# Two-layer GNN kernel: the first half of Wk read in its own rows and transposed by TensorE, and the start's ScalarE and VectorE work in another order

## The chip, the cores and the metric

One core of a Trainium2 chip (trn2). The metric is the time of one execution on the device in microseconds; a kernel's time is the median of its runs. Engines are named as in the profile: PE is TensorE, PEld its weight loads, DVE VectorE, ACT ScalarE, POOL GpSimd, SP SyncE. A `q` behind an engine's name (SPq, ACTq, POOLq) is its sequencer, which issues DMAs, among other things.

## The reference

```python
# x (32, 512, 512), adj (32, 512, 512), nodemask (32, 512) of ones; W0 (512, 1024), Wqk (512, 1024), Wv (512, 512)
# layer 0
h = relu(layernorm(x))
agg = einsum('bij,bjf->bif', adj, h) / max(sum(adj, -1), 1e-6)
x = x + relu(concat([h, agg], 2) @ W0.T)
# layer 1
h = relu(layernorm(x))
q, k = split(h @ Wqk, 2, axis=-1)
v = h @ Wv
a = einsum('bij,bjd->bid', adj, k * mask[:, :, None])
w = mask * einsum('bid,bid->bi', q, a) / sqrt(512)
x = x + softmax(w, axis=1)[:, :, None] * v
```

Everything is float32. q . (adj k) needs Wq and Wk only as M = Wq Wk^T (512 x 512), which the kernel computes once at its start.

## The kernel before

Each of the 32 samples is 512 x 512. Products of 512 x 512 by 512 x 512 are done with seven block products of 256 x 256 instead of eight (`left_sums`, `right_sums` and `product` build the sums before and after). The program is one long list in an order written by hand (a manual schedule): each engine carries out its instructions in the order in which the Python code emits them, and the `Plan` objects place side work between the block products of a phase.

`start()` is the opening, for sample 0 and the weights; the main loop over samples 1 to 31 follows. In `start()`:

- `make_identity` on GpSimd (a memset and an affine select) writes the 128 x 128 identity that TensorE's transposes multiply by. `still` is a zeroed tile for the spare matmuls, five of 128 x 512, which give TensorE work while the weights are on their way.
- DMAs are issued from SP and, where `two_queues` is given, in turn from SP and ACT. `exchange` reads a matrix in pieces of 32 rows, four DMAs (one for each 32 partitions), so that VectorE's 32 x 32 block transposes (`turn_natural`, `turn_ordered`, `turn_right`) make the full transpose of it. Order of issue: Wk's first half (`swk_0`), the four quarters of Wq (`swq_0` to `swq_3`), Wk's second half (`swk_1`), x of sample 0 in two halves, the right half of W0 (`sw2_0`, `sw2_1`), all from both queues; then adj of sample 0 (`fa.load`) and the left half of W0 (`sw1`) from SP alone.
- VectorE, in this order: turn of Wk's first half into `wkT`, of the four quarters of Wq into `wqT`, of Wk's second half; statistics of x's four row chunks (`statistics`, `variance` with its power on GpSimd, `shift`), two chunks and their variance at a time; four turns of W0's right half into `w2R`.
- TensorE: the spare matmuls; M as `multiply(d, h)`, d the row block of 128 and h the half of the columns: (0,0), (1,0), (2,0), (3,0), (0,1), (1,1), (2,1); the transposes of the first two chunks of h = relu(layernorm(x)) (`turn_chunk`); (3,1); then layer 0's first product, `layer0_y(0)`, whose tile is `pp_y`.
- ScalarE: its DMA issues; then `place_m(0)`, `normal(0)`, `normal(1)`, `place_m(1)`, copies of the transposed chunks (`keep_chunk`), and so on. `normal(c)` is relu(x * rstd + nmr), the layernorm of one chunk. Its activation table is loaded ahead of its first activation, `place_m(0)`.

A float32 matmul is carried out as two instructions ("halves"), so a `multiply` is four matmuls and eight halves; a float32 transpose is one instruction. The contraction index of M may be in any order, so long as `wqT` and `wkT` have the same.

Of the kernel before, what the change touches and what calls it, by code (L numbers as in the profile page):

```python
# [16 lines left out]
P = 128  # L17
# [5 lines left out]
def kernel(  # L23
# [11 lines left out]
    nc = tc.nc  # L35
    B, N, F = x.shape
    C = N // P
    H = F // 2
    Q = 4
    R = 32  # L40
# [26 lines left out]
    def mm_tile(name):  # L67
        return ps_m.tile([P, 2, H], F32, tag="m", name=name)
# [10 lines left out]
    def copy(o, i):  # L79
        nc.scalar.activation(o, i, AF.Copy)  # L80
# [107 lines left out]
    def by_rows(src):  # L188

        t = src.rearrange("(q c r) f -> q r c f", q=Q, c=C)  # L190
        return [t[q] for q in range(Q)]
# [8 lines left out]
    one_queue, two_queues = (nc.sync, nc.sync), (nc.sync, nc.scalar)  # L200

    def half_rows(t, src, h, queues=one_queue):
        for q, rows in enumerate(by_rows(src)):
            queues[q % 2].dma_start(out=t[q * R:(q + 1) * R, :, :], in_=rows[:, 2 * h:2 * h + 2, :])

    def exchange(src, name, t=None, queues=one_queue):


        if t is None:
            t = big.tile([P, 8, P], F32, tag="s", bufs=2, name=name)  # L210
        for q in range(Q):
            queues[q % 2].dma_start(
                out=t[q * R:(q + 1) * R, :, :], in_=src[:, :, ts(q, P)].rearrange("k r j -> r k j")
            )
        return t


    mhalf = const.tile([P, C], F32, name="mhalf")
    nc.vector.memset(mhalf, -0.5)

    X, AT_, DEG, W, Y, H1M, H1T, U, TV, HT = ({} for _ in range(10))
# [4 lines left out]
    def room_x(b):  # L226

        t = xu_tile(f"xu_{b}")
        X[b] = t.rearrange("p (c f) -> p c f", c=C)
        U[b] = t.rearrange("p (k i f) -> p k i f", k=4, i=2)  # L230
# [5 lines left out]
    def norm_tiles(name):  # L236
        k = name[0]
        mv = small.tile([P, C, 2], F32, tag=f"mv{k}", name=f"mv{name}")
        rstd = small.tile([P, C], F32, tag=f"rstd{k}", name=f"rstd{name}")
        nmr = small.tile([P, C], F32, tag=f"nmr{k}", name=f"nmr{name}")  # L240
        return mv, rstd, nmr

    def statistics(src, t, c, name):
        st = small.tile([P, 6], F32, tag="st", bufs=4, name=f"st{name}_{c}")
        nc.vector.bn_stats(st, src)
        nc.vector.bn_aggr(t[0][:, c, :], st)

    def variance(t, a=0, b=C):
        mv, rstd, nmr = t
        nc.vector.tensor_scalar(rstd[:, a:b], mv[:, a:b, 1], LN_EPS, None, op0=ALU.add)  # L250
        nc.gpsimd.tensor_tensor(rstd[:, a:b], rstd[:, a:b], mhalf[:, a:b], op=ALU.pow)  # L251

    def shift(t, a=0, b=C):
        mv, rstd, nmr = t
        nc.vector.scalar_tensor_tensor(
            nmr[:, a:b], mv[:, a:b, 0], -1.0, rstd[:, a:b], op0=ALU.mult, op1=ALU.mult
        )
# [463 lines left out]
    w2R, hT = wide[:, 0:7], wide[:, 7:14]  # L721
    tv = const.tile([P, 2, 2, 14, P], F32, name="tv")

    def weight_source(src):
        return src.rearrange("(k r) j -> k r j", r=R)

    def turn_right(t, h, k, dst):

        nc.vector.transpose(
            dst[:, 2 * k + h, :, :].rearrange("p b (k r) -> p k b r", r=R),  # L730
            t[:, :, ts(k, 2 * R)].rearrange("p k (c r) -> p k c r", r=R),
        )

    def turn_ordered(t, d, dst):

        nc.vector.transpose(
            dst[:, :, ts(d, P)].rearrange("p a (k r) -> p k a r", r=R),
            t.rearrange("p k (a r) -> p k a r", r=R),
        )

    def turn_natural(t, h, dst):

        nc.vector.transpose(
            dst[:, :, ts(h, H)].rearrange("p a (k r) -> p k a r", r=R),
            t.rearrange("p k (a r) -> p k a r", r=R),
        )

    mraw = const.tile([P, C, B], F32, name="mraw")
# [29 lines left out]
    def start():  # L778

        H1T[0] = big.tile([P, 7, 7, P], F32, tag="h1T", bufs=1, name="late")  # L780
        late = H1T[0].rearrange("p s i f -> p (s i f)")
        identity = held["identity"] = late[:, 5120:5248]
        make_identity(nc, identity)
        still = late[:, 5248:5248 + 512]
# [4 lines left out]
        HT[1] = spread[:, 3584:7168].rearrange("p (s b f) -> p s b f", s=7, b=2)  # L789
        w1R = spread[:, 0:3584].rearrange("p (s b f) -> p s b f", s=7, b=2)  # L790

        def rows16(n):
            return room[:, n:n + 2048].rearrange("p (k f) -> p k f", f=P)

        sq, sk, s1 = rows16(0), rows16(2048), rows16(7168)
        wk_rows = weight_source(wqk[:, F:2 * F])
        wq_rows = wqk[:, 0:F].rearrange("(q c r) j -> c q r j", q=Q, c=C)
        exchange(wk_rows[0:8], "swk_0", sk[:, 0:8], two_queues)
        for d in range(C):
            exchange(wq_rows[d], f"swq_{d}", sq[:, 4 * d:4 * d + 4], two_queues)  # L800
        exchange(wk_rows[8:16], "swk_1", sk[:, 8:16], two_queues)
        room_x(0)
        for h in range(2):
            half_rows(X[0][:, 2 * h:2 * h + 2, :], x[0], h, two_queues)
        s2 = []
        for h in range(2):
            s2.append(exchange(weight_source(w0[:, F:2 * F])[8 * h:8 * h + 8], f"sw2_{h}", None, two_queues))
        fa = FA[0] = FrontA(0)
        fa.load(0)
        fa.load(1)  # L810
        exchange(weight_source(w0[:, 0:F]), "sw1", s1)
        fh = FH[1] = FrontH(1)
        wqT = late[:, 0:2048].rearrange("p (c f) -> p c f", c=C)
        wkT = late[:, 2048:4096].rearrange("p (c f) -> p c f", c=C)
        mask_sb, mask_by = late[:B, 4096:4608], late[:B, 4608:5120]

        spare = mm_tile("spare").rearrange("p a f -> p (a f)")
        for n in range(5):
            nc.tensor.matmul(spare, still[:, 0:P], still, start=True, stop=True)

        t = norm_tiles("0_0")
        h0 = hT
# [27 lines left out]
        def place_m(d):  # L850
            place(d, 0, held["m", d].rearrange("p a f -> p (a f)"))

        turn_natural(sk[:, 0:8], 0, wkT)
        for d in range(C):
            turn_ordered(sq[:, 4 * d:4 * d + 4], d, wqT)
        turn_natural(sk[:, 8:16], 1, wkT)
        for h in range(2):
            for c in (2 * h, 2 * h + 1):
                statistics(X[0][:, c, :], t, c, "0_0")
            variance(t, 2 * h, 2 * h + 2)  # L860
            shift(t, 2 * h, 2 * h + 2)
        for h in range(2):
            for k in range(2):
                turn_right(s2[h], h, k, w2R)

        for d in range(C):
            multiply(d, 0)
# [33 lines left out]
        p = Plan()  # L901
# [53 lines left out]
        p = Plan()  # L955
# [52 lines left out]
        f = F1[0] = FrontH1(0)  # L1008
# [9 lines left out]
        p = Plan()  # L1018
# [25 lines left out]
        p = Plan()  # L1044
# [22 lines left out]
    }  # L1067
    with tc.manual_schedule(engines=engines):
        weights, mvR = start()
        post = None  # L1070
        for i in range(1, B):
            more, last = i + 1 < B, i + 1 == B
            f = F1[i] = FrontH1(i)
            p = Plan()
# [40 lines left out]
            if 1 < i and i + 2 < B:  # L1115
                fh = FH[i + 2]
                late = i == 2
# [22 lines left out]
            p = Plan()  # L1140
# [53 lines left out]
            p = Plan()  # L1194
# [40 lines left out]
            if more:  # L1235
                p = Plan()
# [25 lines left out]
        p = Plan()  # L1262
# [11 lines left out]
        p = Plan()  # L1274
# [39 lines left out]
```

## Time and profile before

| | |
|---|---|
| runs | 2264.6, 2262.58, 2265.03 us; median 2264.6 |
| the profiled execution | 2263.74 us; span 2262.0 us, 32862 instructions |
| PE busy | 2253.7 us (100% of the span) |
| PEld busy | 1981.3 us (88%) |
| DVE, ACT, POOL busy | 1913.5 (85%), 1024.9 (45%), 175.6 us (8%) |
| granted TensorE clock | 1.00 |
| DMA | 463.69 MB, mean 205 GB/s |
| first spare matmul | 1.48 us after the span's start |
| first matmul of M (`pm`) | 7.79 us |
| ScalarE's table load | 18.58 us, 1.28 us long |
| first `normal` on ScalarE | 20.37 us |
| first matmul of layer 0's product (`pp_y`) | 24.15 us |

The span runs from the first to the last instruction that the profiler saw. In a view of the timeline each row has the start and the length in us, the engine, the line of the kernel, the operation, its output and input tiles, their shapes and how often it stands there; the bracket at the end is the idle time of the engine before it and what ended that. In a view of waits a row has who waited and for whom: us in total, how many times, the longest. The chain is the work that ended last, followed back from the end: start, us, what.

### The profile page before, as it was taken

The numbers are of one execution on the slowest core, as the hardware profiler recorded it, in microseconds if no ns is written. First come the engines' busy times: TensorE is split into PE (matmuls) and PEld (weight loads), VectorE is DVE, ScalarE is ACT, GpSimd is POOL, SyncE is SP. The second block draws the span as 40 slices with busy tenths as digits, with TensorE's granted clock in tenths as the row PEclk, the third lists the DMA queues.
The fourth block names the chain that finished last, engine by engine and source line by source line (L and its number), as shares of the span: only waits on it lengthen the run. The fifth ranks groups of instructions, "written<-read, shape, count | busy, mean of one in ns | idle before, by whom it ended". The sixth has DMA issues, their size and how long they took to land.

```text
span 2262.0 us, 32862 instructions
## 1 busy us (share of the span) xinstructions
PE 2253.7 (100%) x10526; PEld 1981.3 (88%) x10526; DVE 1913.5 (85%) x3778; ACT 1024.9 (45%) x1895; POOL 175.6 (8%) x261
## 2 busy tenths in 40 slices
PE   9999999999999999999999999999999999999999
PEld 7888888888888888888888888888888888888888
DVE  7988888888888888888888888888888888888776
ACT  4454443445434544434454344543444443445323
POOL 0010000000000000000000000000000000000000
PEclk9999999999999999999999999999999999999999
DMA  9988787888877887877878788888778777887644
GB/s 205 252 233 246 208 208 193 205 222 219 209 200 192 212 227 204 207 198 201 233 207 209 198 199 218 221 205 203 194 211 228 203 208 193 205 231 209 156 120 108
DMA packets 409997, 463.69 MB, mean 205 GB/s; under 512 B 38208, under 2 KB 271680, under 8 KB 405600
## 3 DMA queue, kind: packets, MB, share of 16 engines
q1 hardware_dynamic: 396608, 426.46, 69.3%
q0 software_dynamic: 8928, 32.51, 8.8%
q10 hardware_dynamic: 4288, 2.62, 0.6%
q8 instruction: 83, 1.36, 0.3%
q14 instruction: 90, 0.74, 0.1%
HBM read 293.93 MB, written 167.51 MB: 204 GB/s over the span
## 4 chain that ended last, share of the span: by engine, by line
PE 98%; DMA 1%; SPq 0%; ACT 0%; issue 0%; DVE 0%; DVEq 0%
PE ptv L470 28%; PE pp_o L103 19%; PE pp_y L103 10%; PE pp_u L103 10%; PE pq_o L103 9%; PE pq_y L103 5%; PE pq_u L103 5%; PE pr_o L103 5%; PE pr_y L103 2%; PE pr_u L103 2%; PE pw L521 1%; DMA mv<-in_L_gnn_Wqk_dram 0%; PE pp_v L103 0%; PE pp_t L103 0%; DMA w<-dw 0%; DMA xu<-in_x_dram 0%
## 5 line engine op out<-in xcount | busy, mean ns | idle before, releaser
L470 PE MATMUL ptv<-mv,h1T 128*128 128x256 f32 x2842 | 618.4, 379 | 0.0
L470 PEld LDWEIGHTS ptv<-mv,h1T 128*128 128x128 f32 x2842 | 539.9, 190 | 73.7 <-DVE xu L449 0.4
L74 DVE TENSOR_TENSOR tv<-tv 128x256 f32<-128x256 f32 (+1 forms) x645 | 322.0, 511 | 13.2 <-ACT tv L80 1.5
L80 ACT ACTIVATE tv<-ptv 128x512 f32<-128x512 f32 (+1 forms) x360 | 185.0, 541 | 262.9 <-PE ptv L470 261.9
L103 PE MATMUL pp_u<-h1m,aT 128*128 128x256 f32 x1024 | 241.9, 379 | 0.0
L103 PE MATMUL pp_y<-wide 128*128 128x256 f32 x992 | 234.4, 379 | 0.7 <-ACT y L80 0.7
L103 PE MATMUL pp_o<-y,aT 128*128 128x256 f32 x992 | 234.3, 379 | 0.0
L103 PE MATMUL pp_o<-w,wide 128*128 128x256 f32 x960 | 226.8, 379 | 0.0
L103 PEld LDWEIGHTS pp_u<-h1m,aT 128*128 128x128 f32 x1024 | 194.5, 190 | 26.4
L103 PEld LDWEIGHTS pp_y<-wide 128*128 128x128 f32 x992 | 188.3, 190 | 26.6 <-ACT y L80 1.1
L103 PEld LDWEIGHTS pp_o<-y,aT 128*128 128x128 f32 x992 | 188.4, 190 | 25.6
L103 PEld LDWEIGHTS pp_o<-w,wide 128*128 128x128 f32 x960 | 182.4, 190 | 24.8
L80 ACT ACTIVATE o<-pp_o 128x512 f32<-128x512 f32 x96 | 57.3, 597 | 300.1 <-PE pp_o L103 300.1
L80 ACT ACTIVATE y<-pp_y 128x512 f32<-128x512 f32 x124 | 74.0, 597 | 234.0 <-PE pp_y L103 234.0
L74 DVE TENSOR_TENSOR tv<-ptv,tv 128x512 f32<-128x512 f32 x240 | 139.9, 615 | 43.2 <-PE ptv L470 39.6
L80 ACT ACTIVATE xu<-pp_u 128x512 f32<-128x512 f32 x127 | 75.8, 597 | 193.6 <-PE pp_u L103 193.6
L77 DVE TENSOR_TENSOR h1T<-h1T 128x512 f32<-128x512 f32 (+1 forms) x183 | 158.3, 879 | 1.2
L251 POOL TENSOR_TENSOR rstd<-rstd,mhalf 128x2 f32<-128x2 f32 (+1 forms) x97 | 79.8, 823 | 642.5 <-DVE rstd L250 642.5
L103 PE MATMUL pq_u<-h1m,aT 128*128 128x256 f32 x512 | 121.0, 379 | 0.0
L74 DVE TENSOR_TENSOR tv<-ptv,m_tv 128x512 f32<-128x512 f32 (+1 forms) x120 | 72.1, 623 | 56.6 <-PE ptv L470 55.4
L103 PE MATMUL pq_y<-wide 128*128 128x256 f32 x496 | 117.3, 379 | 0.0
L103 PE MATMUL pq_o<-y,aT 128*128 128x256 f32 x496 | 117.2, 379 | 0.0
(173 smaller groups left out, 3354.7 us busy)
## 6 DMA issues: line engine op xcount, KB each, us to landing
w<-dw SPq DMA_DIRECT2D x217, 256.0 KB, 4.2
a<-in_adj_dram SPq DMA_DIRECT2D x256, 128.0 KB, 3.0
dx<-xu SPq DMA_DIRECT2D x32, 1024.0 KB, 5.0
sh1T<-dh1T SPq DMA_DIRECT2D x256, 128.0 KB, 3.4
shT<-dhT SPq DMA_DIRECT2D x248, 128.0 KB, 6.0
daT<-a SPq DMA_DIRECT2D x124, 256.0 KB, 3.0
xu<-in_x_dram SPq DMA_DIRECT2D x124, 256.0 KB, 5.4
dh1T<-h1m SPq DMA_DIRECT2D x124, 256.0 KB, 3.2
```

The costliest lines, as they stand in the source:

```text
L74: (on or nc.vector).tensor_tensor(o, a, b, op=ALU.add)
L77: (on or nc.vector).tensor_tensor(o, a, b, op=ALU.subtract)
L80: nc.scalar.activation(o, i, AF.Copy)
L103: nc.tensor.matmul(p[:, rc, :], lt[:, LEFT[k], dk, ts(rc, P)], right[:, dk, :], start=first and rc == 0 and dk == 0, stop=True, skip_group ...
L251: nc.gpsimd.tensor_tensor(rstd[:, a:b], rstd[:, a:b], mhalf[:, a:b], op=ALU.pow)
L470: nc.tensor.matmul(banks[n][:, :, ts(i, P)], left[:, LEFT[k], LEFT_IN[j], :], mvR[:, RIGHT[k], RIGHT[j], :, :], start=first and i == 0, st ...
L521: nc.tensor.matmul(banks[n][:, ts(i, P)], left[:, LEFT[k], LEFT_IN[j], :], mvR[:, RIGHT[k], RIGHT[j], which, :], start=first and i == 0, s ...
```

## The change

Wk's first half (256 rows) is read in its own rows, 128 rows to a DMA, one DMA from each queue in place of four. `turn_first_wk` transposes it on TensorE, four transposes of 128 x 128 for each group of 128 rows, each taking every fourth column, and ScalarE copies the two results into `wkT`. It stands in the program behind the issue of Wq's third quarter, and on TensorE ahead of the first `multiply`. Since `wkT` now has every fourth index in a chunk, the turns of Wq and of Wk's second half take the same order ("(r a)" in place of "(a r)"). The spare matmuls are two in place of five. A copy of four numbers on ScalarE, behind the issue of Wq's first quarter, brings the table load there. Wk's second half is turned in two steps. x is read from SP alone, and `sw1` in eight DMAs in place of four. VectorE's statistics are interleaved: the second pair's statistics begin before the first pair's shift, and the second's shift stands behind a turn of W0.

```diff
--- before.py
+++ after.py
@@ -735,14 +735,14 @@
 
         nc.vector.transpose(
             dst[:, :, ts(d, P)].rearrange("p a (k r) -> p k a r", r=R),
-            t.rearrange("p k (a r) -> p k a r", r=R),
+            t.rearrange("p k (r a) -> p k a r", r=R),
         )
 
-    def turn_natural(t, h, dst):
+    def turn_natural(t, h, dst, a, b):
 
         nc.vector.transpose(
-            dst[:, :, ts(h, H)].rearrange("p a (k r) -> p k a r", r=R),
-            t.rearrange("p k (a r) -> p k a r", r=R),
+            dst[:, a:b, ts(h, H)].rearrange("p a (k r) -> p k a r", r=R),
+            t.rearrange("p k (r a) -> p k a r", r=R)[:, :, a:b],
         )
 
     mraw = const.tile([P, C, B], F32, name="mraw")
@@ -789,34 +789,48 @@
         HT[1] = spread[:, 3584:7168].rearrange("p (s b f) -> p s b f", s=7, b=2)
         w1R = spread[:, 0:3584].rearrange("p (s b f) -> p s b f", s=7, b=2)
 
+        wqT = late[:, 0:2048].rearrange("p (c f) -> p c f", c=C)
+        wkT = late[:, 2048:4096].rearrange("p (c f) -> p c f", c=C)
+        spare = mm_tile("spare").rearrange("p a f -> p (a f)")
+        for n in range(2):
+            nc.tensor.matmul(spare, still[:, 0:P], still, start=True, stop=True)
+
+        def turn_first_wk():
+            for n in range(2):
+                p = mm_tile(f"wk_{n}").rearrange("p a f -> p (a f)")
+                for a in range(C):
+                    nc.tensor.transpose(p[:, ts(a, P)], wk_first[:, n, a:512:C], identity)
+                copy(wkT[:, :, ts(n, P)], p.rearrange("p (a i) -> p a i", a=C))
+
         def rows16(n):
             return room[:, n:n + 2048].rearrange("p (k f) -> p k f", f=P)
 
         sq, sk, s1 = rows16(0), rows16(2048), rows16(7168)
         wk_rows = weight_source(wqk[:, F:2 * F])
         wq_rows = wqk[:, 0:F].rearrange("(q c r) j -> c q r j", q=Q, c=C)
-        exchange(wk_rows[0:8], "swk_0", sk[:, 0:8], two_queues)
-        for d in range(C):
+        wk_first = sk[:, 0:8].rearrange("p (n k) f -> p n (k f)", n=2)
+        for n in range(2):
+            two_queues[n].dma_start(out=wk_first[:, n], in_=wqk[ts(n, P), F:2 * F])
+        exchange(wq_rows[0], "swq_0", sq[:, 0:4], two_queues)
+        copy(late[:, 5760:5764], mhalf)
+        for d in range(1, C):
             exchange(wq_rows[d], f"swq_{d}", sq[:, 4 * d:4 * d + 4], two_queues)
+            if d == 2:
+                turn_first_wk()
         exchange(wk_rows[8:16], "swk_1", sk[:, 8:16], two_queues)
         room_x(0)
         for h in range(2):
-            half_rows(X[0][:, 2 * h:2 * h + 2, :], x[0], h, two_queues)
+            half_rows(X[0][:, 2 * h:2 * h + 2, :], x[0], h)
         s2 = []
         for h in range(2):
             s2.append(exchange(weight_source(w0[:, F:2 * F])[8 * h:8 * h + 8], f"sw2_{h}", None, two_queues))
         fa = FA[0] = FrontA(0)
         fa.load(0)
         fa.load(1)
-        exchange(weight_source(w0[:, 0:F]), "sw1", s1)
+        for h in range(2):
+            exchange(weight_source(w0[:, 0:F])[8 * h:8 * h + 8], f"sw1_{h}", s1[:, 8 * h:8 * h + 8])
         fh = FH[1] = FrontH(1)
-        wqT = late[:, 0:2048].rearrange("p (c f) -> p c f", c=C)
-        wkT = late[:, 2048:4096].rearrange("p (c f) -> p c f", c=C)
         mask_sb, mask_by = late[:B, 4096:4608], late[:B, 4608:5120]
-
-        spare = mm_tile("spare").rearrange("p a f -> p (a f)")
-        for n in range(5):
-            nc.tensor.matmul(spare, still[:, 0:P], still, start=True, stop=True)
 
         t = norm_tiles("0_0")
         h0 = hT
@@ -850,18 +864,22 @@
         def place_m(d):
             place(d, 0, held["m", d].rearrange("p a f -> p (a f)"))
 
-        turn_natural(sk[:, 0:8], 0, wkT)
         for d in range(C):
             turn_ordered(sq[:, 4 * d:4 * d + 4], d, wqT)
-        turn_natural(sk[:, 8:16], 1, wkT)
-        for h in range(2):
-            for c in (2 * h, 2 * h + 1):
-                statistics(X[0][:, c, :], t, c, "0_0")
-            variance(t, 2 * h, 2 * h + 2)
-            shift(t, 2 * h, 2 * h + 2)
-        for h in range(2):
-            for k in range(2):
-                turn_right(s2[h], h, k, w2R)
+        for a in range(2):
+            turn_natural(sk[:, 8:16], 1, wkT, 2 * a, 2 * a + 2)
+        statistics(X[0][:, 0, :], t, 0, "0_0")
+        statistics(X[0][:, 1, :], t, 1, "0_0")
+        variance(t, 0, 2)
+        statistics(X[0][:, 2, :], t, 2, "0_0")
+        shift(t, 0, 2)
+        statistics(X[0][:, 3, :], t, 3, "0_0")
+        variance(t, 2, 4)
+        turn_right(s2[0], 0, 0, w2R)
+        shift(t, 2, 4)
+        turn_right(s2[0], 0, 1, w2R)
+        for k in range(2):
+            turn_right(s2[1], 1, k, w2R)
 
         for d in range(C):
             multiply(d, 0)
```

## The prediction

> **What bounds the kernel now.** I read the page's busy times and chain first, then the waits of TensorE, then the timeline of the first 25 us engine by engine, and last the instructions of one GpSimd line.
>
> ```profile
> PE 2253.7 (100%) x10526; PEld 1981.3 (88%) x10526; DVE 1913.5 (85%) x3778; ACT 1024.9 (45%) x1895; POOL 175.6 (8%) x261
> ...
> PE 98%; DMA 1%; SPq 0%; ACT 0%; issue 0%; DVE 0%; DVEq 0%
> ```
>
> TensorE is the chain almost from end to end. Its waits from 24 us to the end:
>
> ```profile
> PE pp_y L103 <- ACT y L80: 0.7, 1, 0.7
> PE pp_o L103 <- DMA w<-dw: 0.3, 1, 0.3
> ```
>
> That is 1.0 us in 2238. So whatever moves the first matmul of layer 0's Y (pp_y, 24.15 us) moves the end by as much, and the change touches only what lies ahead of it. The chain there:
>
> ```profile
> 20.47 1.41 ACT h L831 x2
> 21.88 0.04 issue
> 21.93 0.66 PE h L763 x4
> 22.59 1.73 PE pm L839 x8
> 24.31 1.73 PE pp_y L103 x8
> ```
>
> One product `multiply(d, h)` is 8 matmul halves in 1.73 us (0.216 each). Eight products are 13.8 us; the transposes of two chunks of h are 8 at 0.11, 0.9 us; restarts 0.1. So 14.8 us of work lie between the first pm and pp_y. They took 24.15 - 7.79 = 16.36: 1.6 us were waits, nearly all for `normal` on ScalarE, which issued DMAs until 18.34 and then loaded its table (18.58, 1.28 us).
>
> The weight loads of TensorE's first matmuls show its pace:
>
> ```profile
> 4.20 0.34 PEld L819 LDWEIGHTS spare<-late 128*128 128x128 f32 x1 [0.52 <-issue]
> 5.05 0.31 PEld L819 LDWEIGHTS spare<-late 128*128 128x128 f32 x1 [0.52 <-issue]
> 5.60 0.19 PEld L819 LDWEIGHTS spare<-late 128*128 128x128 f32 x1 [0.24 <-issue]
> 6.03 0.19 PEld L819 LDWEIGHTS spare<-late 128*128 128x128 f32 x1 [0.24 <-issue]
> ```
>
> The halves of the spare matmuls stand 0.85 us apart until 5.05 and 0.43 from 5.60 on: at about 5.3 us, 3.8 after the first (1.48), the pace doubles. (The granted clock reads 1.00 throughout and doesn't show this.)
>
> GpSimd's timeline holds what I take to decide the case:
>
> ```profile
> 0.73 0.20 POOL masks.py:197 MEMSET late<- 128x128 f32 x1 [0.29 <-POOLq L1300]
> 8.97 0.28 POOL masks.py:199 TENSOR_SCALAR_AFFINE_SELECT late<-late 128x128 f32<-128x128 f32 x1 [8.04 <-issue]
> 17.87 0.74 POOL L251 TENSOR_TENSOR rstd<-rstd,mhalf 128x2 f32<-128x2 f32 x1 [8.62 <-DVE rstd L250]
> ```
>
> The identity is complete only at 9.25, though its two instructions are first in the program. Before the change nobody reads it until 21.22. The same pause stands elsewhere; of `Post`'s line 342:
>
> ```profile
> L342 POOLq MODIFY_POOL_CONFIG  x60: 83/83/83, 154.3 to 2168.6; - x60
> ...
>   issue: 144.4, 19
> ```
>
> Behind such a configuration GpSimd sits idle for no visible reason, 144.4 / 19 = 7.6 us each (6.8 to 8.9); the one at the start lies at 1.0 us. I therefore expect the same pause in the changed kernel.
>
> **The change, part by part.** *Wk's first half.* Removed: VectorE's turn of 128x1024 (1.25 us) and two DMAs. Added: 8 transposes on TensorE ahead of the first product, and two copies of 128x512 on ScalarE. `multiply(0, 0)` needs both copies, the copies the transposes, and the transposes the identity. The row of a chunk of h gives 0.11 us for a transpose at full pace, with 0.3 from the last start until its result can be read; at half pace I take 0.22. The copy is 0.60 (ACT L80, 0.597 on the page). The start T0 of the products:
> - identity 9.25, transposes 8 x 0.22 = 1.75 and tail 0.3: 11.3; second copy 0.60: 11.9; wake-ups 0.1: T0 = 12.0.
> - at full pace 8 x 0.11 = 0.9: T0 = 11.15.
> The two DMAs (2 KB rows) and swq_0 land well ahead of 9.25 (the eight transfers first issued had landed by 6.9 us before), so they cost nothing.
>
> *Spare matmuls, 5 to 2.* Four halves of 0.85 end at about 5.0. Then TensorE stands idle for over 4 us. The trace has no such gap, so what the pace is afterwards must be bounded: nothing lost (full pace), or the ramp again. The row's ramp of 3.8 us at half pace costs 1.9; a ramp that has to begin twice over costs 3.8. I take 2.4, above the row, since transposes with waits between them come first. With it pp_y starts at 12.0 + 14.8 + 2.4 = 29.2, that is 5.05 us later than before. Ends for this part: 11.15 + 14.8 = 25.95 (1.8 later) and 30.6 (6.5 later).
>
> [...]
>
> *ScalarE's and SP's queues.* ScalarE issues DMAs in program order with its other work, so behind its two copies stand its issues of swq_3, swk_1 and sw2. At most eight transfers are out at once: the ninth issue, at 4.06, waits for the first to land, and so on down both queues:
>
> ```profile
> SPq L212 <- DMA mv<-in_L_gnn_Wqk_dram: 3.3, 5, 1.5
> ...
> SPq L204 <- DMA mv<-in_L_gnn_Wqk_dram: 2.8, 4, 1.0
> ```
>
> So SP's second transfer of x waits for a piece of swq_3 that ScalarE can issue only at 12.0; it lands some 2.7 us later (median of 64 KB), at 14.7. swk_1 lands at about 16.4, two turns of 0.71 end at 17.9, and `multiply(0, 1)` wants it at 21.4. Seven more transfers of x, 0.9 MB at about 215 GB/s, land at 18 (first half) and 20. Statistics 2 x 0.85, 0.17, GpSimd's 0.74 and the shift give `normal(0)` its operands at 20.5, about when ScalarE's last sw2 issue is through; TensorE wants h at 26.6. Nothing of this reaches the path: the smallest slack is 3.5 us (1.1 at full pace).
>
> *Table load early, statistics in another order.* The load (1.28 us) moves to about 2.2 us beside the first transfers, and VectorE no longer stands 0.86 us twice for GpSimd. Together with the shorter queue they would remove the 1.6 us of waits, and the sum above has them removed already (14.8, not 16.36). If their cover fails, at most these 1.6 us come back.
>
> *Strided reads.* The turns of Wq and the transposes now read every fourth element. No row shows such a read. For VectorE's four turns of 0.71, even double lies beside the wait for the identity, so nothing; for the transposes between nothing and double, 0.9 to 1.75 us; I take nothing, as at half pace there is time to read. *Wk's second half in two turns* (1.42 for 1.25): 0.2 us inside 3.5 of slack. *sw1 in eight issues for four:* about 1.5 us of SP's queue. sw1 was read at 35.25, 3.4 us ahead of its last turn and 4.3 ahead of pp_o (39.5); both now move by about 5 us.
>
> Sum: +5.05 us. The profiled execution took 2263.74 (span 2262.0), 0.86 under the median of 2264.6; so 2268.8 against its own time, 2269.6 against the median.
>
> **Rivals.** *A, the identity is early (not slower).* If GpSimd's pause at the start is a matter of that one execution or of how GpSimd's spans are drawn, transposes start when Wk lands, about 5.2. The copies then follow ScalarE's seventh issue, T0 is about 7.1, (2, 1) ends at 19.3, and h's first chunk comes at 19.75 and the second at 20.4, since ScalarE is still held by sw2's issues until 18.3: pp_y at about 22.7, 1.45 earlier, 2263.1. It decides when the identity is complete before some 7.4 us. Against it: 19 pauses of the same kind in this trace, none under 6.8.
> *B, TensorE keeps full pace* through the gap: T0 11.15, pp_y 25.95, +1.8, 2266.4. For it: the pauses up to 1.25 us before lost nothing. Against: this one is over three times as long, and two spares end before the 5.3 us at which the pace doubled.
> *C, the transfers fall behind as well.* ScalarE's queue stands from about 6.4 to 12, in which some 1 MB less is moved (5 us at 210 GB/s). The stage after is nearly saturated; if adj's halves then come later than TensorE's own delay, ScalarE's sums wait and its copies behind them. Two us more: +7, 2271.6.
>
> **How the numbers follow.** A measurement of this kernel can tell about 0.2% (4.5 us) from no change. Forecast 0.66, of which 0.1 has a loss of pace small enough to stay under 4.5; C 0.05; B 0.17; A 0.10; something faster that I don't see 0.02. Slower: 0.56 + 0.05, about 0.60; same: 0.38; faster: 0.02. The range runs from B with the identity 1 us earlier (2265.4) to the forecast with the longest pause (+0.9) and the longest ramp (+1.4), 2272.0; outside lie A and the unseen.
>
> **What would show it.** Right: the affine select near 9 us and the first transpose of Wk behind it, waiting for GpSimd; the first pm at 11 to 12, its halves 0.43 apart for some us; ScalarE's swq_3 issue at about 12; pp_y near 29. Wrong: transposes before 7 us, or pm halves at 0.216 from the first.

## The result, and the profile after

The changed kernel takes 2268.45 us in the median of 22 runs, the kernel before 2264.2 in 22: 4.25 us more, a ratio of 1.0018 with a 95% interval of 1.0012 to 1.0024. The profiled execution took 2267.56 us, its span 2265.8.

The page of the changed kernel, engines and chain by engine:

```profile
PE 2254.1 (99%) x10528; PEld 1983.2 (88%) x10528; DVE 1914.5 (84%) x3778; ACT 1026.3 (45%) x1898; POOL 175.6 (8%) x261
...
PE 99%; issue 0%; ACT 0%; DVE 0%; POOL 0%; DVEq 0%; POOLq 0%
```

DMA has left the chain and GpSimd has come into it. The chain of the opening says where (start, us, what):

```profile
0.98 0.01 POOLq masks.py:199
0.99 8.48 issue
9.47 0.29 POOL late masks.py:199
9.76 0.04 issue
9.81 2.00 PE wk L802 x8
11.81 0.02 issue
11.83 0.61 ACT late L80
12.44 0.04 issue
12.48 14.38 PE pm L853 x56
26.86 0.87 PE h L763 x8
27.74 1.73 PE pm L853 x8
29.47 1.73 PE pp_y L103 x8
```

Up to 9.76 us the chain is GpSimd: its configuration (the row of POOLq), 8.5 us of nothing that the profile shows, the affine select. Then come the eight transposes of Wk, the second copy, and TensorE without a pause to layer 0's product. TensorE's waits in the first 40 us (waiter, releaser: us, times, longest):

```profile
PE wk L802 <- POOL late masks.py:199: 4.5, 1, 4.5
...
PE pm L853 <- ACT late L80: 0.7, 1, 0.7
```

The pace shows in a count of TensorE's matmul halves in two stretches of 3.9 us:

```profile
12.50:16.40 3.90, 3.90 (x9) 1.00 0.71 190
16.80:20.70 3.90, 3.90 (x20) 1.00 1.16 243
```

The columns after the stretch are its length, busy us with the number of halves under way in it, granted clock, DMA share and GB/s. The count takes in halves that began just before the stretch; 8 began inside the first and 18 inside the second. Both stretches are "busy" throughout, both at a granted clock of 1.00: the first runs at half pace, and neither busy time nor granted clock says so.

### The profile page after: what moved, and what is told of

Same layout as the page of the kernel before. It is cut to its first block, busy times and chain, and to the rows that moved or that the text cites. A ratio compares the mean times of both kernels' runs of the same rounds, so it can differ in the third digit from the quotient of the medians.

```text
span 2265.8 us, 32879 instructions
## 1 busy us (share of the span) xinstructions
PE 2254.1 (99%) x10528; PEld 1983.2 (88%) x10528; DVE 1914.5 (84%) x3778; ACT 1026.3 (45%) x1898; POOL 175.6 (8%) x261
## 4 chain that ended last, share of the span: by engine, by line
PE 99%; issue 0%; ACT 0%; DVE 0%; POOL 0%; DVEq 0%; POOLq 0%
PE ptv L470 28%; PE pp_o L103 20%; PE pp_y L103 10%; PE pp_u L103 10%; PE pq_o L103 10%; PE pq_y L103 5%; PE pq_u L103 5%; PE pr_o L103 5%; PE pr_y L103 2%; PE pr_u L103 2%; PE pw L521 1%; PE pm L853 1%; PE pp_v L103 0%; PE pp_t L103 0%; PE pq_t L103 0%
```

## Experiments

Theory 1 was that of the forecast: the identity's lateness, with the pace that TensorE loses while it waits, is the whole cost. Theory 2: the path of the transposition itself (strided reads, copies in ScalarE's queue) costs. Theory 3: the transfers held behind ScalarE's copies cost. Each kernel stands against runs of the kernel before on the same chip; pp_y is the first matmul of layer 0's product in the profiled execution (before 24.15, after 29.30). Each pp_y is that of one execution: e8 and e12 are the same kernel and stand at 23.04 and 23.47.

| run | first pm, us | pp_y, us | median, us | before, us | ratio, 95% interval |
|---|---|---|---|---|---|
| changed kernel | 12.48 | 29.30 | 2268.45 | 2264.2 | 1.0018 [1.0012, 1.0024] |
| e1_vector_identity | 8.40 | 23.84 | 2263.12 | 2263.95 | 0.9995 [0.9985, 1.0004] |
| e2_vector_identity_4_spares | 8.82 | 24.99 | 2262.64 | 2263.95 | 0.9995 [0.9986, 1.0005] |
| e3_rest_alone | 7.86 | 24.24 | 2263.48 | 2263.95 | 0.9997 [0.9988, 1.0007] |
| e4_transpose_alone | 12.34 | 29.43 | 2268.98 | 2263.95 | 1.0022 [1.0013, 1.0032] |
| e5_ten_spares | 14.62 | 29.41 | 2267.69 | 2264.09 | 1.0015 [1.0006, 1.0024] |
| e6_copies_later | 12.85 | 30.70 | 2268.13 | 2264.09 | 1.0018 [1.0009, 1.0027] |
| e7_table_and_statistics | 8.58 | 23.27 | 2264.0 | 2264.09 | 1.0001 [0.9992, 1.0009] |
| e8_rest_x_two_queues | 7.86 | 23.04 | 2262.57 | 2264.09 | 0.9994 [0.9986, 1.0003] |
| e9_six_spares | 12.00 | 26.79 | 2265.83 | 2263.8 | 1.0008 [0.9999, 1.0018] |
| e10_sw1_in_eight | 8.12 | 23.20 | 2262.51 | 2263.8 | 0.9994 [0.9985, 1.0003] |
| e11_e8_sw1_in_four | 7.77 | 22.82 | 2263.41 | 2263.8 | 0.9999 [0.999, 1.0008] |
| e12_e8_again | 8.78 | 23.47 | 2263.2 | 2263.8 | 0.9996 [0.9987, 1.0005] |

### The identity from VectorE

```diff
-        make_identity(nc, identity)
         still = late[:, 5248:5248 + 512]
         nc.vector.memset(still, 0.0)
+        col, row = late[:, 5776:5808], late[:, 5808:5840]
+        nc.vector.memset(col[:, 0:1], 0.0)
+        for s in (1, 2, 4, 8, 16):
+            nc.vector.tensor_scalar(col[:, s:2 * s], col[:, 0:s], float(s), None, op0=ALU.add)
+        nc.vector.transpose(row, col)
+        nc.vector.memset(identity, 0.0)
+        for q in range(Q):
+            b = slice(q * R, (q + 1) * R)
+            nc.vector.tensor_tensor(identity[b, b], col[b], row[b], op=ALU.is_equal)
```

> The changed kernel, with the identity built by VectorE in about 2 us (done near 3.5 us) and nothing else altered. Theory 1 (the identity's late arrival, with the pace lost while TensorE stood still, is the whole cost): the transposes of Wk start when its two DMAs land, near 6 us; the copies stand behind ScalarE's issue that ended at 7.7 us in the changed kernel, and the first turn of Wq ended there at 8.1, so the first pm is at 8.9 us, not 12.5. First matmul of layer 0's product at 23.7 us if the pace is full by then, at 25.6 us with a ramp of 4 us at half pace: 2263.7 to 2265.7, 3 to 5 us under the changed kernel. Theory 2 (the path of the transposition itself costs: strided reads, copies in ScalarE's queue): the first pm comes no earlier than 11 us and the kernel stays within 1.5 us of the changed one's 2268.4.

Measured: 2263.12 us, 5.3 under the changed kernel and 0.8 under its own runs of before, which is within the noise. TensorE's timeline of the opening (start, us, line, form, count, idle before and what ended it):

```profile
5.24 1.96 PE L810 MATMUL wk<-late,mv 128*128 128x128 f32 x8
8.40 7.17 PE L861 MATMUL pm<-late 128*128 128x256 f32 x32 [1.21 <-ACT late L80]
15.84 5.56 PE L861 MATMUL pm<-late 128*128 128x256 f32 x24 [0.26 <-DVE late L743]
```

The transposes begin when Wk lands, 4.6 us sooner, and 24 halves take 5.56 us, full pace. Nothing but the maker of the identity was altered, so the identity's lateness, with the pace lost behind it, carries the whole loss; theory 2 falls as an account of it. A part of theory 2 stays: the first pm is still 0.6 later than in the kernel before (7.79), held by the copies behind ScalarE's issues.

> As e1_vector_identity, with four spare matmuls in place of two, so that TensorE is at work until about 6.9 us and at full pace from 5.3 on. It shows what the pace alone is worth where the identity is early. Theory 1: transposes at 0.11 us from 6.9 us, first pm at 8.9 with its halves 0.216 apart from the first, first matmul of layer 0's product at 23.7 us, 2263.7, so 0.5 under the kernel before; and under e1 by whatever ramp e1 shows (0 to 2 us). If the pause from 7.8 to 8.9 us lowers the pace again, it is no faster than e1. Theory 2: within 1.5 us of the changed kernel's 2268.4.

Four spares (`range(4)` for `range(2)` in the loop of spare matmuls): transposes 0.12 us apart from 7.01, pm at full pace from 8.82; 2262.64, no difference from e1 that these runs can tell. In this execution TensorE waited 1.0 us for the turns of Wk's second half (DVE L743). Since e1 already had full pace at its first pm, hardly any ramp was left to save: only its transposes ran at half pace (1.96 us against 1.12).

### The two halves of the change, each alone

```diff
 # e3: the changed kernel, but
-        for n in range(2):
-            two_queues[n].dma_start(out=wk_first[:, n], in_=wqk[ts(n, P), F:2 * F])
+        exchange(wk_rows[0:8], "swk_0", sk[:, 0:8], two_queues)
 ...
-            if d == 2:
-                turn_first_wk()
 ...
+        turn_natural(sk[:, 0:8], 0, wkT, 0, C)
         for d in range(C):
             turn_ordered(sq[:, 4 * d:4 * d + 4], d, wqT)
 # turns in the order "(a r)", five spares
```

> The changed kernel without the transposition: Wk's first half read in four pieces and turned by VectorE first of all, contiguous reads in the turns, five spare matmuls; the early table load, x from SP alone, the second half's turn in two steps and the new order of statistics stay. Theory 1 with the forecast's claim that the rest takes away the 1.6 us of waits before layer 0's product: first pm at 7.8 us, ScalarE free at about 18 us without a table load behind it, first matmul of layer 0's product at 22.7 us in place of 24.15, 2262.8, that is 1.4 us under the kernel before. Rival: x from SP alone lands later and gives the gain back: 24.2 us and 2264.2.

For pp_y the rival is right: 24.24 us. The time, 2263.48 us, lies between the two. ScalarE is free early, and then stands (timeline of ScalarE in e3):

```profile
17.61 0.60 ACT L855 ACTIVATE mv<-pm 128x512 f32<-128x512 f32 x1 [13.44 <-DMA xu<-in_x_dram]
20.45 1.52 ACT L841 ACTIVATE h<-xu,nmr,rstd 128x512 f32<-128x512 f32 x2 [2.24 <-DVE nmr L255]
```

2.24 us idle until the shift of x's statistics; those began at 17.21 in e3, at 15.87 in the kernel before. With x from both queues again, and nothing else altered:

```diff
-            half_rows(X[0][:, 2 * h:2 * h + 2, :], x[0], h)
+            half_rows(X[0][:, 2 * h:2 * h + 2, :], x[0], h, two_queues)
```

> e3_rest_alone with one thing altered: x read from both queues as in the kernel before. Theory (x from SP alone is what cost e3 its gain): x's first half lands 1 us or more earlier than in e3, layer 0's product begins at 22.8 us in place of e3's 24.24, about 2262.3. Rival: x's time of landing is set by the bytes ahead of it and not by who issues it: product at 24.0 to 24.3, within 0.3 us of e3.

The same two rows of ScalarE in e8:

```profile
18.65 0.60 ACT L855 ACTIVATE mv<-pm 128x512 f32<-128x512 f32 x1 [14.47 <-DMA sw<-in_L_gnn_W_dram]
19.24 1.52 ACT L841 ACTIVATE h<-xu,nmr,rstd 128x512 f32<-128x512 f32 x2
```

`normal(0)` starts 1.2 us sooner without a wait, pp_y at 23.04. x's statistics begin at 16.28, 0.9 sooner. So reading x from SP alone takes back, at pp_y, what the early table load and the order of statistics give. The times of e3, e8 and e12 (0.9997, 0.9994 and 0.9996 of their own runs of before) don't tell them apart.

```diff
 # e4: the kernel before, and
-        exchange(wk_rows[0:8], "swk_0", sk[:, 0:8], two_queues)
+        for n in range(2):
+            two_queues[n].dma_start(out=wk_first[:, n], in_=wqk[ts(n, P), F:2 * F])
         for d in range(C):
             exchange(wq_rows[d], f"swq_{d}", sq[:, 4 * d:4 * d + 4], two_queues)
+            if d == 2:
+                turn_first_wk()
 ...
-        turn_natural(sk[:, 0:8], 0, wkT)
 # turns in the order "(r a)", two spares
```

> The kernel before with the transposition alone (Wk's first half in its own rows, transposed by TensorE, copied by ScalarE, two spare matmuls, turns in the strided order); x from both queues, statistics, sw1 and the second half's turn as before. Theory 1: identity at 9.3 to 9.8 us, first pm at 12.5 with some 4 us at half pace, first matmul of layer 0's product at 29.3 us as in the changed kernel, 2268.4, since the waits that the rest of the change removes are hidden behind TensorE's delay anyway. Rival (the parts add up): 1.4 us slower than the changed kernel, 2269.8.

29.43 us and 2268.98, as the changed kernel: the transposition alone makes the whole loss. Its waits of TensorE are the changed kernel's, too:

```profile
PE wk L802 <- POOL late masks.py:199: 4.4, 1, 4.4
...
PE pm L850 <- ACT late L80: 0.7, 1, 0.7
```

### The pace

`range(10)`, then `range(6)`, for `range(2)` in the changed kernel's loop of spare matmuls.

> The changed kernel with ten spare matmuls in place of two, which keep TensorE at work from 1.5 to about 10 us, a little past the identity (9.3 to 9.8). It splits the 5.2 us by which layer 0's product began later into the wait for the identity and the loss of pace. Theory 1: transposes at 0.11 us from about 10.0, first pm at 11.8 and its halves 0.216 apart from the first, first matmul of layer 0's product at 26.6 in place of 29.3; so about 2266, 2.5 us under the changed kernel and 2 over the kernel before. Rival: the pace falls in the 0.8 us in which TensorE waits for ScalarE's copies, or spare matmuls of zeros don't hold it: halves 0.43 apart for 4 us, no faster than the changed kernel, 2268.4.

This missed its aim. The pace doubled at about 6.9 us in that execution and not at 5.3, so the spares lasted until 12.8 and hid the identity's wait behind themselves (first pm 14.62). It shows still that TensorE, once at full pace there, kept it through the transposes (8 in 1.12 us) and the 0.7 us wait for the copies (25 halves of pm in 5.66 us).

> The changed kernel with six spare matmuls in place of two. Ten had kept TensorE at work until 12.7 us, past the identity, so they hid what they were to show; six end between 8.5 and 9.3 us, ahead of the identity, whether the pace doubles at 5.3 or at 6.9 us. Theory 1: transposes at 0.11 us from 9.3 to 9.8, first pm at 11.1 to 11.6 with its halves 0.216 apart from the first, first matmul of layer 0's product at 25.9 to 26.4 in place of 29.3; about 2266, which is the forecast's other end for the pace. Rival: the pace falls in the pauses before and behind the transposes, no faster than 2268.

```profile
1.48 8.05 PE L796 MATMUL spare<-late 128*128 128x512 f32 x12 [1.48 <-DVE late L785]
10.07 1.23 PE L802 MATMUL wk<-late,mv 128*128 128x128 f32 x8 [0.54 <-POOL late masks.py:199]
12.00 12.35 PE L853 MATMUL pm<-late 128*128 128x256 f32 x56 [0.69 <-ACT late L80]
```

The identity came at 10.02 in this execution. The transposes took 1.23 us where the changed kernel's took 1.98, the 56 halves 12.35 where those took 14.38. pp_y is at 26.79, 2.5 sooner, and the time is 2.4 us lower against its own runs of before (+2.0 in place of +4.25). So about half of the loss is pace, the rest is waiting. That split rests on the traces: the interval of e9's ratio (0.9999 to 1.0018) would allow a loss from nothing to 4 us.

### The queue behind ScalarE's copies

```diff
-            if d == 2:
-                turn_first_wk()
         exchange(wk_rows[8:16], "swk_1", sk[:, 8:16], two_queues)
+        turn_first_wk()
```

> The changed kernel with the copies of the transposed half of Wk put behind ScalarE's issues of swq_3 and swk_1 (ahead of x and sw2), so that these four transfers no longer wait for the identity. Theory 1 (what the queues hold up has slack): those four issues end near 10 us and not at 13.6, x lands 1 to 3 us earlier, the first pm stays near 12.4 and layer 0's product at 29.3, 2268.4 within 0.7. Theory 3 (the transfers held behind ScalarE's copies cost part of the 4 us): 1 us or more faster, 2267.4 or less.

ScalarE's four issues now end at 9.3 us and x's statistics begin at 15.6 in place of 18.0; the time is 2268.13, 4.0 over its own runs of before. A row each from the timelines of ScalarE and TensorE in e6:

```profile
6.70 2.61 ACTq L212 DMA_DIRECT2D mv<-in_L_gnn_Wqk_dram  x5
12.85 15.41 PE L852 MATMUL pm<-late 128*128 128x256 f32 x56 [0.69 <-ACT late L80]
```

The times alone couldn't exclude theory 3's 1 us, but the trace of the changed kernel does: from 12.48 us to pp_y TensorE doesn't pause once, so nothing on its path waited for those transfers. Theory 3 falls: that backlog had slack. (pp_y is 1.4 later in e6's profiled execution: 1.0 because its half pace lasted 6.2 us, 0.4 because its identity came at 10.13.)

### Whether an earlier start is kept

```diff
 # e7: the kernel before, with
+            if d == 0:
+                copy(late[:, 5760:5764], mhalf)
 # and VectorE's new order of statistics, shifts and turns of W0
```

> The kernel before with two parts of the change alone: ScalarE's table load early and the new order of h's statistics and shifts. x from both queues, Wk as before. If e3_rest_alone gained nothing because x from SP alone landed later, then here h's first chunk can be made at about 19.0 us in place of 20.4, layer 0's product begins at 22.8 in place of 24.15, and the kernel takes about 2262.6, 1.3 under the kernel before. If instead the statistics' order is what holds (the first shift stands behind the third chunk's statistics, which wait for x's second half), product at 24 us and no gain.

pp_y came 0.9 us earlier and the time stayed. TensorE's waits from 24 us on:

```profile
PE pp_o L103 <- DMA w<-dw: 0.8, 2, 0.5
PE pp_y L103 <- ACT y L80: 0.7, 1, 0.7
```

The stream load of W1 (w from dw) takes back most of it near 90 us (0.75 us; 0.4 goes at 75 and 87 us). e7 differs from e8, which keeps its early start, in the issues of sw1 above all. e10 is e7 with sw1 in eight issues, e11 is e8 with it in four, e12 is e8 once more:

```diff
-        exchange(weight_source(w0[:, 0:F]), "sw1", s1)
+        for h in range(2):
+            exchange(weight_source(w0[:, 0:F])[8 * h:8 * h + 8], f"sw1_{h}", s1[:, 8 * h:8 * h + 8])
```

> e7_table_and_statistics with sw1 in eight issues in place of four, which leaves as its differences from e8_rest_x_two_queues the order of the two queues' pieces and the second half's turn in two steps. e7 began layer 0's product 0.9 us earlier than the kernel before and ended with it, for TensorE waited 0.8 us for a stream load of W1 (w from dw) near 90 us. If sw1's issues decide that, no such wait and 2262.6; if it is chance or another part of e8, e10 stays at 2264.0.

> e8_rest_x_two_queues with sw1 in four issues as before. If sw1's issues decide whether an earlier start is kept to the end, the wait for the stream load near 90 us returns and the kernel takes about 2264; if not, 2262.6 as e8.

> e8_rest_x_two_queues once more, beside e10 and e11 on one chip, as the version that is to beat both kernels: 2262.6, 1.5 us under the kernel before; with the 11 runs of the first time its gain is then told with 20 runs or more. If the first time was chance, 2263.5 to 2264.

With sw1 in eight issues 2262.51 (e10), 2262.57 (e8) and 2263.2 (e12); in four 2264.0 (e7) and 2263.41 (e11). The profiled executions agree with that order: set beside the kernel before, matmul for matmul, the two with four issues lose 1.2 us (e7) and 1.3 (e11) of their early start between 30 and 90 us, and e8, e10 and e12 lose none there. In e11 pp_y is the earliest of all (22.82), but TensorE's last matmul comes only 0.7 us earlier than before; in e10 it comes 1.45 earlier, more than the 0.95 of its pp_y, because a wait of the kernel before near 110 us is missing. That points at sw1, but the medians lie within 1.5 us of each other and e12 was 0.6 above e8, the same kernel: it stays open. So does a version that beats both kernels: e10 and e8 are 1.3 to 1.5 us under the kernel before in their medians, and the intervals of their ratios, 0.9985 to 1.0003 and 0.9986 to 1.0003, both hold 1. All of e1, e2, e3, e7, e8, e10, e11 and e12 are faster than the changed kernel.

## Why the prediction was right

The cause, the order and most sizes were right; the time lies in the range, 1.15 us under the forecast of 2269.6 (4.25 us over the kernel before in place of 5.0). The measured 0.19% (interval 0.12 to 0.24) lies on the 0.2% that it had taken as the bound between same and slower, so it doesn't say which of these two, with chances of 0.38 and 0.60, came true.

- *GpSimd's pause.* Identity forecast at 9.25, measured at 9.75; the executions with `make_identity` range from 9.25 to 10.1. The pause behind the configuration is there in each of them, 8.0 to 8.9 us; what fills it no run shows.
- *T0.* 12.0 forecast, 12.48 measured: 0.5 from the identity, while 8 transposes at half pace (0.213 apart) and the copy (0.60) came as worked out.
- *Work between pm and pp_y.* 16.82 us measured, of which 2.0 are lost pace (56 halves in 14.38 us, where e9's took 12.35); 14.8 remain, as the sum had it.
- *Loss of pace.* 2.4 forecast, 2.0 measured, close to the row of before (1.9). That is partly luck: the 2.4 was a choice between nothing and 3.8, and the loss differs by execution (2.3 in e4, 3.1 in e6, which take the same path). Counted from the first spare, or from the first pm where TensorE had stood still, half pace lasted 3.3 us (e11), 3.8 (before), 4.1 (changed kernel), 4.7 (e4), 5.4 (e5), 5.9 (e12) and 6.2 (e6). So these runs spread over 2.9 us and show no fixed time; what raises the pace they don't show. In e1 the spares end at 5.1, the transposes are still at half pace at 6.8 (8 in 1.96 us), and pm is at full pace from 8.40 (32 halves in 7.17 us): there it doubled with nothing behind the spares but the transposes and a wait of 1.21 us.
- *Queues.* ScalarE's swq_3 issue forecast at 12.0, 11.84 measured; x's halves at 18 and 20, statistics at 17.99 and 20.04. That none of it reaches the path, TensorE's unbroken run to pp_y shows and e6 agrees.

pp_y was forecast 5.05 us later and came 5.15 later. The terms that failed:

- *The whole shift reaches the end.* Of the 5.15 us at pp_y 4.47 are left at TensorE's last matmul and 3.8 in the time of the two profiled executions (4.25 between the medians). 0.45 go near 110 us, where the kernel before waited for a stream load and the changed one did not; this line of the chain of before has no fellow in the chain after:

```profile
104.67 5.24 DMA w<-dw
```

  At that place the shift shrinks from 5.15 to 4.70, at 188 us to 4.47, and so it stays to the last matmul. The forecast saw the 0.3 us wait and took it for a constant, which it isn't. Whether a late start is what removes it stays open: e4, e5, e6 and e9, which start late, lack it, but so do e2, e3, e10, e11 and e12, which begin pp_y between 1.3 us earlier and 0.8 later than the kernel before; all nine come 0.5 to 0.55 us forward at the same matmul. So the wait may belong to the one profiled execution of the kernel before. The last 0.65 lie behind the last matmul, a stretch of 5.3 us in the kernel before, 4.6 in the changed one and 4.6 to 5.4 in the others.
- *"Together with the shorter queue they would remove the 1.6 us of waits."* Behind a late TensorE nobody could see it, and the sum was right; by itself it is wrong, as e3 showed (24.24): with x from SP alone its statistics begin at 17.21, 1.3 us later than in the kernel before and 0.9 later than in e8. Without that edit pp_y comes 1.1 us (e8) or 0.7 (e12) earlier than before.
- *Strided reads.* "Even double" was the bound; the turn went from 0.71 to 1.10 us, the transpose from 0.11 to 0.12 at full pace; at half pace it took 0.213, no more than twice the contiguous 0.109. VectorE's turns (min/median/max ns) in the changed kernel:

```profile
L736 DVE STREAM_TRANSPOSE late<-mv x4: 1082/1096/1122, 7.0 to 14.4; 128x512 f32<-128x512 f32 x4
```

  In the changed kernel the wait for the identity covers them; in e1 and e2, where it is gone, TensorE waits for such a turn (0.3 and 1.0 us).
- *Rival A's size.* It gave T0 7.1, pp_y 22.7 and 2263.1. e1 measured 8.40, 23.84 and 2263.12: the start was 1.3 too early, since the copies stand behind ScalarE's issue that ends at 7.2 and go one after the other. That the time agrees so well is luck.

## What to carry to other kernels

Before an engine is given work earlier, look for the operand that nobody has needed so early until now: here the identity, first in the program and ready only at 9.25 us, which cost nothing so long as its first reader came at 21. Look at the releaser's own timeline, not at its place in the code. And read a matmul's spacing, not TensorE's busy time or granted clock, when TensorE has stood still: here the halves of pm stood 0.43 us apart and later 0.216, both at a granted clock of 1.00, and about half the loss (2.5 of the 5.15 us at pp_y, by e9) was pace.

## What the runs showed of the hardware

- Behind the configuration at the start of GpSimd's program (1.0 us) the affine select began only at 9.0 to 9.9 us in every profiled execution that had one (8.0 to 8.9 us idle). Memsets of GpSimd ahead of it ran at 0.25 to 0.73 us. What fills the pause no run shows.
- The moment at which TensorE's pace doubles differs from execution to execution, with the same matmuls from 1.48 us on: 5.3 us in the kernel before and in e8, about 6.9 in e5, e7 and e9, 4.8 in e11, 7.4 in e12, which is e8's kernel. Where the spares then last longer, they hold up the work they were put ahead of: e7's five ended late and its first pm came at 8.58.
- A float32 block transpose on VectorE that reads every fourth element took 1.10 us for 128x512 against 0.71 contiguous; on TensorE the transposes at the same stride stood 0.12 us apart at full pace, contiguous ones 0.109.
